# Transfers of a hybrid Mamba, SSD and mixture-of-experts kernel: the experts' reload issued by ScalarE, SSD row loads by quads in one DMA, a pair's decays in one DMA

## The chip, the cores and the metric

The kernel runs on one core of a Trainium2 chip. Its five engines each work through their own list of instructions in order: TensorE (PE in the profile, with its weight loads as PEld), VectorE (DVE), ScalarE (ACT), GpSimd (POOL) and SyncE (SP), which issues most of the DMAs. The metric is the device time of one execution in microseconds; lower is better. Three executions of the kernel before took 849.16, 842.12 and 846.15 us, with a median of 846.15 us.

## The reference

The input x is 4 sequences of 512 tokens with 256 features, all float32. Four blocks follow each other, each with a layer norm in front and its result added to x:

```python
x = x + _L0_attn_a_ref(_layernorm(x, axis=-1), ...)   # selective scan (Mamba), 16 states
x = x + _L0_ffn_ref(_layernorm(x, axis=-1), ...)      # mixture of 8 experts, top 2
x = x + _L0_attn_b_ref(_layernorm(x, axis=-1), ...)   # chunked state-space block (SSD)
x = x + _L0_ffn_ref(_layernorm(x, axis=-1), ...)      # the same mixture, same weights
```

The change lies in the SSD block and in what the last block needs. The SSD block has 64 heads of 8 features and 64 states, and cuts time into chunks of 32:

```python
dA = (dt * A).reshape(b, c, CHUNK, H)
Acs = jnp.cumsum(dA, axis=2)
Lm = jnp.exp(_segsum(jnp.moveaxis(dA, 3, 2)))
Y_diag = jnp.einsum('bclhn,bcshn,bchls,bcshp->bclhp', Ch, Bh, Lm, xd)
decay_states = jnp.exp(Acs[:, :, -1:, :] - Acs)
states = jnp.einsum('bclhn,bclh,bclhp->bchpn', Bh, decay_states, xd)
chunk_decay = jnp.exp(Acs[:, :, -1])
...
_, prev = jax.lax.scan(step, h0, (jnp.moveaxis(chunk_decay, 1, 0), jnp.moveaxis(states, 1, 0)))
Y_off = jnp.einsum('bclhn,bchpn,bclh->bclhp', Ch, prev, jnp.exp(Acs))
```

In the mixture every expert is computed for every token, `h = jnp.einsum('td,edf->etf', xf, expert_w) + expert_b`, then weighted by the router's top two.

## The kernel before, in words

The kernel keeps x in SBUF and runs the four blocks over the four sequences ("batches" b = 0 to 3). In the time of the profile the selective scan fills about the first 320 us, the first mixture (names ending in `_e`) runs beside and after it to about 440 us, the SSD block (names ending in `_s`) from about 440 to 710 us, and the last mixture (`_f`) from there to the end.

**The SSD block.** The heads of a batch are worked in four groups g of 16 heads, and the groups in two pairs p. `front_b` (from L1648) makes for each batch the running sums of the decay exponents (`cs`) and writes the lower rows of both halves to DRAM (`cs_rows`, L1664); it also writes the decays over whole chunks (`dk_rows`, L1680). `weighted` (L1775) then does, for each group: the weighted x is written to DRAM (`x_rows`), and the group's rows of `cs_rows` are read back into a tile `less` in another layout, 16 chunk partitions by 32 steps, two parts of four heads' quads each (L1791 to L1798). `apart` (L1801) reads `x_rows` back, by chunks, in four DMAs into one of two tiles `x_b`. `states` (L1811) does, for each pair: it reads `dk_rows` into two tiles `decays` (one for each half h of a group's heads), each copied to all 64 partitions of a group (L1819 to L1826); TensorE makes the states (`pst`), ScalarE copies them to `starts`, VectorE scans them over the 16 chunks with the decays (`starts<-decays_s_p,starts`), and TensorE multiplies them with C (`po_s_p`). `decayed` makes for each quad q a matmul with `less` (`pe_s`), an exponential and a product (`m_s`); `within` multiplies that with `x_b` (`pz_s<-x_b,m_s`). The tiles `decays` have two buffers in all, so those of a pair are free when the scans of the pair before are done.

**The experts' weights.** The weights of the mixture are split into high and low parts once (`load_moe`), kept in DRAM after the first mixture (`keep_moe`, L849), and read back into the space that the SSD block's front has left, when the front of the last batch is done (`reload_moe`, L858): `expert_h` and `expert_l` of 2 MB each, `expert_b` of 1 MB copied to all partitions, and four small tensors.

**What sets the order.** Every operation is recorded by a planner (class `Plan`, L209 on), which orders all engines' instructions by costs of its own and then issues them; all of them appear as line L612, its last line. It prices a DMA by its bytes alone (`n.cost = max(b / 360e3, 0.112)`, L656), whatever its shape and the number of its pieces. So an edit to a DMA can move instructions all over the program.

**How DMAs are held apart.** The program has eight semaphores for DMAs, given out in turn in the program's order, to SP's and ScalarE's DMAs alike. Before a DMA is issued, its engine waits until the DMA that had the same semaphore before, eight places earlier, has landed. An engine that waits so does nothing else.

Of the kernel before, what the change touches and what calls it, by code (L numbers as in the profile page):

```python
# [22 lines left out]
F32 = mybir.dt.float32  # L23
# [7 lines left out]
P = 128  # L31
# [7 lines left out]
DI, NH, HD, DS = 512, 64, 8, 64  # L39
# [16 lines left out]
BL, NB = 32, P // 32  # L56
# [14 lines left out]
def bc(ap, axis, n):  # L71

    a = ap.unsqueeze(axis)
    shape = list(a.shape)
    shape[axis] = n
    return a.to_broadcast(shape)
# [641 lines left out]
def block(ctx: ExitStack, tc: Plan, a: dict, out: bass.AP):  # L718
    nc = tc.nc
    V, S, G, T = nc.vector, nc.scalar, nc.gpsimd, nc.tensor  # L720
# [22 lines left out]
    def bank(tag, name, shape=(P, L)):  # L743

        if tag == "mm":
            return banks.tile(list(shape), F32, tag=tag, name=name)
        at = turn[tag] = turn.get(tag, -1) + 1
        names = PAIRS.get(tag, tag.split())
        return banks.tile(list(shape), F32, tag=names[at % len(names)], name=name, bufs=1)
# [6 lines left out]
    def load(b):  # L756
# [8 lines left out]
        out=ident, in_=ident, compare_op=ALU.is_equal, fill=0.0, base=0, pattern=[[-1, P]], channel_multiplier=1  # L765
# [49 lines left out]
        S.copy(hi, src)  # L815
        low.tensor_tensor(lo, src, hi.bitcast(F32), ALU.subtract)

    def load_bias(w):
        flat = a["expert_b"].rearrange("e f -> (e f)")
        nc.sync.dma_start(out=w["expert_b"], in_=flat.partition_broadcast(P))  # L820

    def load_moe(w, raw):
        load_bias(w)
# [32 lines left out]
        return kept  # L856

    def reload_moe(w, kept):  # L858
        for key, t in kept.items():
            nc.sync.dma_start(out=w[key].bitcast(F32), in_=t)  # L860
        load_bias(w)

    def row(rows, at, name):
        lo, hi = at[name]
# [253 lines left out]
    for t in range(0, 4, 2):  # L1118
        for k in range(KB):
            nc.scalar.dma_start(  # L1120
                out=conv_w[:, k, t : t + 2], in_=a["conv_w"][t : t + 2, k * P : (k + 1) * P, :].rearrange("t p o -> p t o")
# [8 lines left out]
        out=a_neg.rearrange("p j g -> p (j g)"), in_=a["A_log"].rearrange("(n d) j g -> d n (j g)", d=BL)  # L1130
# [12 lines left out]
    def ltile(shape, name):  # L1143
        return later.tile(shape, F32, tag=name, name=name)
# [26 lines left out]
    for j in range(2):  # L1171
        t = ltile([P, 4, P], f"less_all{j}")
# [3 lines left out]
        flat = t[BL:NH].rearrange("p q c -> p (q c)")  # L1176
# [221 lines left out]
    for b in range(B):  # L1398
# [13 lines left out]
        for k in range(KB):  # L1412
# [3 lines left out]
            for j in range(2):  # L1416
                for r, name in zip(pairs[2 * k + j], "du"):
                    t = m_p.tile([P, 2, L], F32, tag=f"{name}s", name=f"{name}s_{b}_{k}_{j}", bufs=SPREAD)
                    spread.append(t)
                    if b == k == 0:  # L1420

                        for h in range(2):
                            c = slice((2 * j + h) * BL, (2 * j + h + 1) * BL)
# [5 lines left out]
                        out=t.rearrange("p j t -> p (j t)"), in_=bc(r.rearrange("d j t -> d (j t)"), 1, NS)  # L1429
# [61 lines left out]
    at = SSD_AT  # L1491
# [156 lines left out]
    def front_b(b):  # L1648

        nm, small, rot, d_a, zs, xs, wt, ld = made_a.pop(b)  # L1650

        pcs = bank(FRONT_BANKS if b == 0 else "mm", f"pcs_{nm}")
        for i in range(NT):
            T.matmul(
                pcs[:, i * P : (i + 1) * P], d_a[:, i].rearrange("p a c h -> p (a c h)"), upto_b,
                start=True, stop=True,
            )
        cs_rows = dram.tile([2, NH, L], F32, tag="cs_rows", name=f"cs_rows_{nm}")
        cs = c_s[b % 2]
        for a in range(2):  # L1660
            src, lo = pcs[a * NH : (a + 1) * NH], a * NH + NH // 2
            S.copy(cs[a][NH:], src)
            V.tensor_tensor(cs[a][NH + NH // 2 :], pcs[lo : lo + NH // 2], cs[a][NH + NH // 2 :].bitcast(F32), ALU.subtract)
            nc.sync.dma_start(out=cs_rows[a], in_=cs[a][NH:].bitcast(F32))  # L1664
            V.tensor_copy(
                tot[b % 2][a * NH // 2 : (a + 1) * NH // 2, 1:],
                src[: NH // 2].rearrange("p (k l) -> p k l", l=BL)[:, :-1, BL - 1],
            )

        pc = bank(FRONT_BANKS if b == 0 else "mm", f"pc_{nm}")  # L1670
        T.matmul(pc[:, : L // 2], upto_b, d_a[:, :, :, 0, :], start=True, stop=True)
        T.matmul(pc[:, L // 2 :], after_b, d_a[:, :, :, 0, :], start=True, stop=True)
        ends = s_o.tile([P, 2, NT, NH], F32, tag="ends", name=f"ends_{nm}")
        S.activation(ends.rearrange("p c i h -> p (c i h)"), pc, AF.Exp)

        nk = NT * NB
        over_blocks = small("over_blocks", (NH, HD, nk))
        S.activation(over_blocks, bc(tot[b % 2], 1, HD), AF.Exp)
        dk_rows = dram.tile([NH, HD * nk], F32, tag="dk_rows", name=f"dk_rows_{nm}")
        nc.sync.dma_start(out=dk_rows, in_=over_blocks.rearrange("p d k -> p (d k)"))  # L1680
        yield


        nh = NT * NB // 2
        bt = small("rest", (P, L))
        cm = c_m[b % 2]
        for g in range(2):
            pt = bank(FRONT_BANKS if b == 0 else "mm", f"pbc_{nm}_{g}")
            for i in range(NT):
                T.transpose(pt[:, i * P : (i + 1) * P], rot[:, i, g].rearrange("p c n -> p (c n)"), ident)  # L1690
            S.copy(bt if g == 0 else cm, pt)
        bm = b_m[b % 2]
        S.copy(bm, rot[:, :, 0, 0, :])
        gm = s_o.tile([P, nh, 2, BL], F32, tag="gm", name=f"gm_{nm}")
        pg = bank(FRONT_BANKS if b == 0 else "mm", f"pg_{nm}")
        for k in range(nk):
            ks = slice(k * BL, (k + 1) * BL)
            for h in range(4):
                T.matmul(pg[h * BL : (h + 1) * BL, ks], bt[:, ks], cm[:, ks], start=True, stop=True)
        S.activation(gm.rearrange("p j c l -> p (j c l)"), pg, AF.Copy, scale=0.5)  # L1700
        dg = small("tsin", (P, NT, DS))
        V.tensor_tensor(dg, rot[:, :, 0, 0, :], rot[:, :, 1, 0, :], ALU.mult)
        dd = small("dd", (P, NT))
        V.tensor_reduce(dd, dg, AX.X, ALU.add)
        V.tensor_tensor(ld, ld, bc(dd, 2, NH), ALU.mult)
        ready[b] = dict(
            nm=nm, zs=zs, y=xs, wt=wt, ld=ld, ends=ends, dk_rows=dk_rows, gm=gm, cm=cm, bm=bm, cs=cs, cs_rows=cs_rows
        )
# [61 lines left out]
    def per_head(t):  # L1770
        return t.rearrange("p i (h d) -> p i h d", d=HD)
# [3 lines left out]
    def weighted(b, g):  # L1775

        c = ready[b]
        nm = f"{c['nm']}_{g}"
        ch, hs = slice(g * P, (g + 1) * P), slice(g * 16, (g + 1) * 16)
        xs = c["y"][:, :, ch]  # L1780
        xw = pool2.tile([P, NT, P], F32, tag="xw", name=f"xw_{nm}", bufs=1)
        G.tensor_tensor(per_head(xw), per_head(xs), bc(c["wt"][:, :, hs], 3, HD), ALU.mult)
        x_rows = dram.tile([L, P], F32, tag="x_rows", name=f"x_rows_{nm}", bufs=4)
        nc.sync.dma_start(out=x_rows.rearrange("(i p) f -> p i f", p=P), in_=xw)
        xe = pool2.tile([P, NT, P], F32, tag="xe", name=f"xe_{nm}", bufs=XE_BUFS)
        G.tensor_tensor(per_head(xe), per_head(xw), bc(c["ends"][:, 1, :, hs], 3, HD), ALU.mult)

        G.tensor_tensor(per_head(xs), per_head(xs), bc(c["ld"][:, :, hs], 3, HD), ALU.mult)
        nk = NT * NB
        ls = less[g]  # L1790
        for part in range(2):  # L1791
            for q in range(4):
                lo = part * NH // 2 + g % 2 * 16
                src = c["cs_rows"][g // 2, lo + q : lo + 16 : 4, :]
                nc.sync.dma_start(
                    out=ls[part * nk : (part + 1) * nk, q, :].bitcast(F32).rearrange("k (h s) -> k h s", h=4),
                    in_=src.rearrange("h (k s) -> k h s", s=BL),
                )  # L1798
        units[b, g] = dict(xe=xe, x_rows=x_rows, less=ls)

    def apart(b, g):  # L1801
# [9 lines left out]
    def states(b, p):  # L1811

        c = ready[b]
        nm = f"{c['nm']}_p{p}"
        nk = NT * NB
        pair = (2 * p, 2 * p + 1)
        half = [slice(h * DS, (h + 1) * DS) for h in range(2)]
        G.memset(starts[:, :, 0], 0.0)
        decays = []  # L1819
        for h in range(2):  # L1820
            t = pool2.tile([P, P // 2 * nk], F32, tag="decays", name=f"decays_{nm}_{h}")
            for j, g in enumerate(pair):
                at = 16 * g + 8 * h
                src = c["dk_rows"][at : at + 8, :].rearrange("h d -> (h d)")
                nc.sync.dma_start(out=t[half[j]], in_=src.partition_broadcast(DS))
            decays.append(t)  # L1826


        for r0 in range(0, NB, 2):
# [13 lines left out]
            for r in range(r0, r0 + 2):  # L1843
                n = NT if r + 1 < NB else NT - 1
                at = starts[:, :, r + 1 : r + 2 + NB * (n - 1) : NB]
                S.copy(at.rearrange("p c i -> p i c"), pts[r - r0][:, :n, :])
            yield
        for h in range(2):
            at = starts[:, h * P // 2 : (h + 1) * P // 2, :].rearrange("p c k -> p (c k)")
# [83 lines left out]
    order = [(b, g) for b in range(B) for g in range(4)]  # L1933
    coming, going, moe_f, before = [], [], [], None
    weighted(0, 0)
    weighted(0, 1)
    for n, (b, g) in enumerate(order):
# [28 lines left out]
        if g % 2 == 0:  # L1966
            mine = states(b, g // 2)
# [77 lines left out]
```

## Time and profile before

| what | value |
|---|---|
| three executions, median | 846.15 us (842.12 to 849.16) |
| the profiled execution: its time, its span | 836.37 us, 834.7 us |
| PE busy | 709.5 us, 85% of the span |
| DVE busy | 683.8 us, 82% |
| ACT busy | 523.4 us, 63% |
| POOL busy | 527.2 us, 63% |
| granted TensorE clock, mean | 0.894 |
| HBM read and written | 49.67 MB and 16.80 MB |
| less<-cs_rows_s | 128 DMAs of 8 KB, 2.8 us from issue to landing |
| decays_s_p<-dk_rows_s | 32 DMAs of 256 KB, 4.3 us |
| x_b<-x_rows_s | 64 DMAs of 64 KB, 2.4 us |

The profiled execution took 836.37 us; its span, from the first to the last instruction, is 834.7 us. All stretches below are counted from the span's start. In the lists, "SPq" is SP as the issuer of DMAs. A row of a timeline has start, duration, engine, line, operation and tiles, the number of merged instructions, and in brackets the idle time before it and what ended it. A row of the list of waits has who waited, for whom, the total, the number of waits and the longest one, in us. In the list of DMA issues the last number is the median time from issue to landing.

### The profile page before, as it was taken

What the parts mean: (1) busy time and instruction counts of PE and PEld (TensorE: products, weight loads), DVE (VectorE), ACT (ScalarE), POOL (GpSimd) and SP (SyncE); (2) the same over time, 40 slices, a digit from 0 to 9 for tenths busy, and PEclk for the clock granted to TensorE, in tenths of its full rate; (3) what the DMA queues carried; (4) which work ended last, traced back from release to release, by engine and by line L of the source; (5) the groups of instructions that cost most, each with busy time, mean ns of one, the idle gap of its engine ahead of it and who ended that gap; (6) DMA issues with size and microseconds to landing.
All of it is one profiled execution on the core that took longest, in us unless ns stands there. A gap on an engine that the chain in (4) does not pass through costs nothing.

```text
span 834.7 us, 16400 instructions
## 1 busy us (share of the span) xinstructions
PE 709.5 (85%) x6194; PEld 457.5 (55%) x6194; DVE 683.8 (82%) x1278; ACT 523.4 (63%) x965; POOL 527.2 (63%) x410
## 2 busy tenths in 40 slices
PE   8889879966676789799997697789789886999996
PEld 5333324221022247587886475676567664888784
DVE  7488999999999984898996678697677546799987
ACT  2898976865345486566687455645636544686764
POOL 5735857767767574655555886863862873558555
PEclk9989999976577699999999599899789778999999
DMA  8321252241341002600004522521531584000001
GB/s 273 117 76 64 71 184 64 92 162 64 101 176 51 1 7 57 273 1 0 2 5 112 116 64 60 112 65 38 117 80 32 131 264 101 1 1 26 25 2 51
DMA packets 79247, 67.55 MB, mean 81 GB/s; under 512 B 48696, under 2 KB 66040, under 8 KB 78400
## 3 DMA queue, kind: packets, MB, share of 16 engines
q1 hardware_dynamic: 77664, 65.35, 27.2%
q10 hardware_dynamic: 1504, 1.15, 0.5%
q8 instruction: 49, 0.80, 0.4%
q14 instruction: 30, 0.25, 0.1%
HBM read 49.67 MB, written 16.80 MB: 80 GB/s over the span
## 4 chain that ended last, share of the span: by engine, by line
PE 35%; DVE 15%; ACT 8%; SPq 5%; issue 5%; POOL 3%; DMA 1%; POOLq 0%; ACTq 0%; DVEq 0%
PE ph_e L612 8%; PE ph_f L612 6%; SPq L612 5%; PE pz_s L612 4%; DVE hs L612 3%; PE px_s L612 3%; PE po_s L612 2%; DVE starts L612 2%; PE pst_s_p L612 2%; DVE bx L612 1%; PE po_s_p L612 1%; ACT L610 1%; ACT ph_e L612 1%; PE pe_s L612 1%; DVE ph_f L612 1%
## 5 line engine op out<-in xcount | busy, mean ns | idle before, releaser
L612 POOL TENSOR_TENSOR hs<-hs,cb 128x1024 f32<-128x1024 f32 x64 | 151.8, 2380 | 73.8 <-DVE hs L612 61.1
L612 DVE TENSOR_TENSOR_SCAN hs<-da,bx 128x512 f32<-128x512 f32 x128 | 150.5, 1213 | 8.3 <-ACT da L612 5.8
L612 ACT ACTIVATE da<-ds,a_neg 128x512 f32<-128x512 f32 x128 | 87.5, 689 | 76.8 <-DVE hs L612 76.6
L612 PE MATMUL ys<-hs,over 128*32 128x512 f32 x256 | 73.7, 755 | 27.9 <-POOL hs L612 27.9
L612 DVE TENSOR_TENSOR bx<-us,pb 128x1024 f32<-128x1024 f32 x64 | 76.3, 1211 | 0.2
L612 POOL TENSOR_TENSOR m_s<-m_s,gm_s 128x512 f32<-128x512 f32 x32 | 45.3, 1421 | 32.8 <-ACT m_s L612 32.7
L610 ACT ACT_TABLE_LOAD x51 | 65.4, 1283 | 0.9
L612 PE MATMUL pconv<-hh,conv 128*128 128x512 f32 x128 | 60.8, 622 | 1.1 <-ACT hh L612 1.1
L612 ACT ACTIVATE ph_f<-ph_f 128x512 f32<-128x512 f32 x64 | 37.5, 588 | 26.9 <-DVE ph_f L612 26.6
L612 DVE TENSOR_TENSOR ph_f<-ph_f,expert_b 128x512 f32<-128x512 f32 x64 | 43.9, 694 | 11.7 <-DMA expert_b<-in_expert_b_dram 5.7
L612 ACT ACTIVATE ph_e<-ph_e 128x512 f32<-128x512 f32 x64 | 36.8, 586 | 23.7 <-DVE ph_e L612 15.9
L612 PE MATMUL ph_e<-expert_h,xs_of_xh_e 128*128 128x512 f32 x128 | 44.9, 413 | 4.2 <-ACT c_e L612 4.2
L612 PE MATMUL pe_s<-c_s,less 128*128 128x512 f32 x64 | 32.9, 544 | 16.2 <-DMA less<-cs_rows_s 7.4
L612 PEld LDWEIGHTS ys<-hs,over 128*32 128x32 f32 x256 | 8.8, 118 | 66.9 <-POOL hs L612 51.9
L612 POOL TENSOR_TENSOR c_e<-c_e,hb_e 128x512 f32<-128x512 f32 x16 | 20.6, 1290 | 36.1 <-ACT hb_e L612 36.1
L612 PEld LDWEIGHTS pconv<-hh,conv 128*128 128x128 f32 x128 | 24.1, 196 | 34.4 <-issue 28.1
L612 ACT COPY starts<-pst_s_p 128x512 f32<-128x512 f32 (+1 forms) x32 | 29.6, 1010 | 18.3 <-PE pst_s_p L612 18.3
L612 PE MATMUL pz_s<-x_b,m_s 128*32 128x32 f32 x2048 | 31.9, 216 | 10.0 <-DMA x_b<-x_rows_s 5.7
L612 DVE TENSOR_TENSOR_SCAN starts<-decays_s_p,starts 128x1024 f32<-128x1024 f32 x16 | 38.9, 2439 | 1.5 <-issue 1.3
L612 PEld LDWEIGHTS pz_s<-x_b,m_s 128*32 128x32 f32 x2048 | 26.3, 127 | 23.4 <-issue 15.3
L612 PE MATMUL ph_f<-expert_h,xh_f 128*128 128x512 f32 x96 | 38.4, 400 | 0.7 <-ACT c_f L612 0.7
L612 PE MATMUL ph_f<-expert_l,xh_f 128*128 128x512 f32 x96 | 38.4, 400 | 0.0
(399 smaller groups left out, 2163.2 us busy)
## 6 DMA issues: line engine op xcount, KB each, us to landing
decays_s_p<-dk_rows_s SPq DMA_DIRECT2D x32, 256.0 KB, 4.3
ds<-d_rows SPq DMA_DIRECT2D x14, 512.0 KB, 3.8
us<-u_rows SPq DMA_DIRECT2D x14, 512.0 KB, 3.9
cb<-c_rows SPq DMA_DIRECT2D x16, 256.0 KB, 3.3
x_rows_s<-xw_s SPq DMA_DIRECT2D x16, 256.0 KB, 3.0
x_b<-x_rows_s SPq DMA_DIRECT2D x64, 64.0 KB, 2.4
x<-in_x_dram SPq DMA_DIRECT2D x4, 512.0 KB, 4.7
raw_expert<-in_expert_w_dram SPq DMA_DIRECT2D x4, 512.0 KB, 7.1
```

Of the source, the lines that this page charges most:

```text
L610: self.real.scalar.preload_act_table_set(n.table)
L612: n.inst = f(*[self.swap(v) for v in n.args], **{k: self.swap(v) for k, v in n.kw.items()})
```

## The change

There are three edits. The reload of `expert_h`, `expert_l` and `expert_b` goes from SP to ScalarE, in ScalarE's own DMA queue; the four other tensors of the reload stay on SP. The rows of `cs_rows` are written in another order, by four DMAs of 16 rows where there was one of 64, so that the read into `less` takes one DMA for a part where it took four. A pair's decays for one half are read by one DMA into all 128 partitions, where there were two of 64 partitions.

```diff
-    def load_bias(w):
+    def load_bias(w, queue=nc.sync):
         flat = a["expert_b"].rearrange("e f -> (e f)")
-        nc.sync.dma_start(out=w["expert_b"], in_=flat.partition_broadcast(P))
+        queue.dma_start(out=w["expert_b"], in_=flat.partition_broadcast(P))
...
     def reload_moe(w, kept):
+
         for key, t in kept.items():
-            nc.sync.dma_start(out=w[key].bitcast(F32), in_=t)
-        load_bias(w)
+            (S if "expert" in key else nc.sync).dma_start(out=w[key].bitcast(F32), in_=t)
+        load_bias(w, S)
...
-            nc.sync.dma_start(out=cs_rows[a], in_=cs[a][NH:].bitcast(F32))
+
+            for at in range(0, NH, 16):
+                nc.sync.dma_start(
+                    out=cs_rows[a, at : at + 16].rearrange("(q h) l -> h q l", h=4),
+                    in_=cs[a][NH + at : NH + at + 16].bitcast(F32),
+                )
...
         for part in range(2):
-            for q in range(4):
-                lo = part * NH // 2 + g % 2 * 16
-                src = c["cs_rows"][g // 2, lo + q : lo + 16 : 4, :]
-                nc.sync.dma_start(
-                    out=ls[part * nk : (part + 1) * nk, q, :].bitcast(F32).rearrange("k (h s) -> k h s", h=4),
-                    in_=src.rearrange("h (k s) -> k h s", s=BL),
-                )
+            lo = part * NH // 2 + g % 2 * 16
+            nc.sync.dma_start(
+                out=ls[part * nk : (part + 1) * nk].bitcast(F32).rearrange("k q (h s) -> k (q h) s", s=BL),
+                in_=c["cs_rows"][g // 2, lo : lo + 16, :].rearrange("h (k s) -> k h s", s=BL),
+            )
...
             t = pool2.tile([P, P // 2 * nk], F32, tag="decays", name=f"decays_{nm}_{h}")
-            for j, g in enumerate(pair):
-                at = 16 * g + 8 * h
-                src = c["dk_rows"][at : at + 8, :].rearrange("h d -> (h d)")
-                nc.sync.dma_start(out=t[half[j]], in_=src.partition_broadcast(DS))
+            src = c["dk_rows"].rearrange("(g c h) d -> g c (h d)", c=2, h=8)[2 * p : 2 * p + 2, h]
+            nc.sync.dma_start(out=t, in_=bc(src, 1, DS))
             decays.append(t)
```

The new decays DMA has as its source 2 rows, each repeated 64 times, of 1,024 elements; its destination has 128 partitions of 1,024. In the built program the planner puts nearly every engine's instructions in another order than before, from the second sequence of the first block on.

## The prediction

> **What bounds the kernel now.** I read first the page's chain of work that ended last, then the time by stretch, one for each batch of the SSD block, then who waited for which DMA, then the DMA issues, and at last single stretches of the timelines. The chain is mostly TensorE (35%) and VectorE (15%), with SP as issuer at 5%, some 45 us. Work per batch of the SSD block:
>
> ```profile
> 440.00:505.00 65.00, 50.87 (x856) 38.86 (x856) 43.10 (x86) 38.64 (x73) 46.59 (x38) 0.84 0.42 95
> 505.00:573.00 68.00, 56.07 (x1141) 44.71 (x1140) 57.91 (x88) 37.60 (x73) 45.30 (x37) 0.92 0.31 69
> 573.00:640.00 67.00, 56.78 (x1016) 43.11 (x1016) 48.27 (x77) 36.70 (x69) 39.22 (x33) 0.87 0.33 73
> 640.00:710.00 70.00, 56.63 (x1232) 42.70 (x1231) 37.85 (x74) 35.95 (x61) 45.24 (x37) 0.80 0.59 157
> ```
>
> After the length, these columns begin with PE's busy time. PE is busy 51 to 57 of 65 to 70 us in each batch: it is the stage's bound, with 10 to 14 us idle per batch. Only that idle time can be won by faster transfers, and it has several owners. The list of waits gives what the edited DMAs and `x_b` behind them cost PE, and what SP's own big loads cost SP:
>
> ```profile
> PE pe_s L612 <- DMA less<-cs_rows_s: 7.4, 4, 5.8
> PE pz_s L612 <- DMA x_b<-x_rows_s: 5.7, 3, 2.9
> ...
> SPq L612 <- DMA expert_l<-kept_expert_l: 5.4, 1, 5.4
> SPq L612 <- DMA expert_h<-kept_expert_h: 4.9, 1, 4.9
> ```
>
> So 13.1 us of PE's idle time ends on a DMA of SP's queue; 45 us of the chain is SP only because the chain goes back through a queue in which PE's work hides most.
>
> **Row loads by quads.** They take 128 issues of 427 ns (median of the tile's view); 32 remain, so 96 x 0.47 us (with the gap between two) = 45 us of SP time go. The writes of `cs_rows` rise from 8 to 32, 24 x 0.5 = 12 us. The 16 decays issues that go had a median of 574 ns: 9 us. SP wins 42 us, 10 per batch, in the bursts ahead of `x_b`. On the path that is at most the 13.1 us above, of which 5.8 (the longest) belongs to the last batch and the experts' loads; I count a gain of 6 us in batches 0 to 2 and put the rest into the last batch. The new read has 256 runs of 128 bytes, half of an `x_b` read's 512, which takes 487 ns to issue and lands in 2.4 us: no loss there.
>
> **The decays in one DMA.** This is where I expect the loss.
>
> ```profile
> q1 hardware_dynamic: 77664, 65.35, 27.2%
> ...
> decays_s_p<-dk_rows_s SPq DMA_DIRECT2D x32, 256.0 KB, 4.3
> ...
> us<-u_rows SPq DMA_DIRECT2D x14, 512.0 KB, 3.9
> ```
>
> (The q1 row is SP's queue: packets, MB, share of 16 engines.) What no row shows is a DMA of this form: outermost count 2 in the source, 128 in the destination. Lower bound: it is spread like `us`, also 512 KB, 3.9 us. Upper bound: few DMA engines carry it. The trace records each DMA engine's update of a DMA's semaphore. DMAs whose outermost counts are 16 or more (`cb`: 32 in the source, 128 in the destination) leave 16 updates. The two DMAs of four rows, at 23.7 and 33.5 us, leave five: one right at the issue and four at the landing. So the number of engines follows the outermost count, and I take 2. A DMA engine's price for 4 KB: q1 used 0.272 x 16 x 834.7 = 3,633 engine us for 65.35 MB, 55.6 us per MB, so 0.262 MB (half of 512 KB) takes 14.6 us; the faster half of the packets of 4,096 bytes took 159 ns, and 64 of them 10.2 us. With 2 us from issue to landing as for a small DMA: 12 to 17 us instead of 4.3. I take 12, since the rest of the queue is light.
>
> The Trainium skill speaks on both sides here. "DMA: Bandwidth & Descriptors", in the section "Why a DMA increments its semaphore by 16 and not by 1", says that the largest number up to 16 that divides the outermost counts of both sides is the number of engines, which makes the decays use 2 and leaves the sum as it is here. The same page, in "Rules for kernel authors", says of two transfers to disjoint halves of the partitions "Use one 128-partition transfer", by which the edit could only win and the sum would be that of the first rival below.
>
> The scans themselves have room. In batch 1 the decays were issued from 526.26 to 530.29 and the first scan began at 542.86:
>
> ```profile
> 542.86 2.82 DVE L612 TENSOR_TENSOR_SCAN starts<-decays_s_p,starts 128x1024 f32<-128x1024 f32 x1
> ```
>
> The two DMAs of a pair share the two engines, so the second lands 2 + 2 x 10.2 = 22.4 us after the first's issue. That the scans bear within 0 to 3 us. What they do not bear is everything behind the decays in SP's queue: a sixteenth of each `x_rows`, `x_b` and `less` DMA goes over the same two engines and stands in line. PE takes `x_b` as it lands:
>
> ```profile
> 537.79 0.45 PE L612 MATMUL pz_s<-x_b,m_s 128*32 128x32 f32 x16 [2.11 <-DMA x_b<-x_rows_s]
> ```
>
> By batch, with the new order of SP's queue and the old times:
>
> - Batch 0: decays now stand after the second `x_rows` (issued at 466.18) and before the second `x_b`. They are issued at 466.7 and end at 489; PE used that `x_b` from about 475. Loss 13 us.
> - Batch 1: a decays DMA stands on each side of `x_rows` of group 2, which POOL has ready at 527.6. The second ends at about 541, `x_b` lands at 543; it was used at 537.8. Loss 5 us.
> - Batch 2: both stand before that `x_rows`. With the shorter queue they are issued at about 587 and end at 609.4; `x_b` lands 2.4 us later at 611.8, and was used at 605.14. Loss 7 us.
>
> **The experts' reload on ScalarE.** The three issues cost ACT 3 x 0.43 us. The wait costs more. By the eight semaphores in turn, `expert_b` has that of `expert_l`, so ACT stands until `expert_l` has landed. The trace shows that time on SP:
>
> ```profile
> 665.55 0.43 SPq L612 DMA_DIRECT2D expert_h<-kept_expert_h  x1
> ...
> 666.59 0.42 SPq L612 DMA_DIRECT2D expert_l<-kept_expert_l  x1
> 667.05 2.61 SPq L612 DMA_DIRECT2D less<-cs_rows_s  x5
> 674.65 1.09 SPq L612 DMA_DIRECT2D decays_s_p<-dk_rows_s  x2
> 681.17 1.71 SPq L612 DMA_DIRECT2D less<-cs_rows_s  x4
> ```
>
> SP stood at 669.7 for `expert_h` and at 675.7 for `expert_l`, 15.6 us from the first issue to 681.17. ACT will stand for those 15 us with this queued behind: a copy `yh_s`, an exponential of `pe_s`, one of `m_s` and the first copies of `starts`. PE can go on with some 4 us (the output product of a tile of batch 2 and one or two `pe_s`), then it stands too: 10 to 12 us. SP is not freed either: a `cs_rows` write now has the semaphore of `expert_h`. Behind it in SP's queue stand the other decays of the pair, issued some 20 us after the first, so they land 12 us later still. The pair's first scan, at 662.97 before, ends up at about 686. For the second pair `x_b` of group 3 stands between the two decays: PE is through `po_s_p` and `pz_s` of the last pair at about 725 where it was at 706.8, with some 3 us more of `ph_f` done by then. I take 15 us for the last batch, everything counted, the 5.8 us that go included. The last mixture keeps PE busy 56 of the last 65 us, so nothing is made up there.
>
> **The sum.** 13 + 5 + 7 + 15 = 40 us, less 6 for the shorter queue, less 6 because after each stall some of PE's other idle time is gone (VectorE and POOL have run ahead): +28 us. The moved order of the first 440 us I count at nothing; it could be some 6 us either way, a tenth of PE's 66 idle us there. The profiled execution of 836.37 us would become 864; the median of 846.15, 10 us above it, becomes 874.
>
> **Rivals.** (1) Faster: the decays DMA is spread over all 16 engines. Then it lands in about 5 us, all 13 us of PE's waits go, and the stand of ACT is covered by PE's queue: 846 - 13 = 833 us. It decides if a decays DMA lands within some 6 us. For it speaks the `us` row; against it the four-row DMAs. (2) No change: the decays are slow, but the two engines take turns between DMAs, so `x_b` lands in 4 or 5 us, and the scans' room covers the decays. Then the loss is ACT's stand, 10 us, against 10 won: 846 us, 840 to 853. For it speaks the room of 8 us and more ahead of most scans; against it, that `x_b` waits on the decays only if each engine works in order of issue, which no row shows. (3) Worse: at 14.6 us for each half of a decays DMA, a pair takes 31 us where a pair's time is 33. Then scans and `x_b` are both late by 9 us more in each batch: 874 + 31 = 905 us.
>
> **Chances.** Forecast 0.68, rival 1 0.07, rival 2 0.13, rival 3 0.12. A measurement of this kernel can't tell less than about 1% from no change, so faster means under 838 and slower over 854.5 us: 0.07, 0.13 and 0.80. The forecast's own range, with the bounds of the batches' losses, is 856 to 895. To leave out no more than 2 in 10 the range goes from 848, the middle of rival 2, to 903, the near end of rival 3.
>
> **What will show it.** In the profile after, a decays DMA's time to landing should be 12 us or more, and `x_b`'s longest well over the 8.9 us of before. PE's waits for `x_b` or for what stands before it should grow to 20 us or more. ACT should have one gap of about 15 us just after the issue of `expert_l`. SP should have 32 `less` issues and more time in waits than in issues. I would be wrong if decays land in 4 to 6 us, or if ACT's gap falls where PE has work, or if the new order by itself moves the first 440 us by more than 6 us.

## The result, and the profile after

The changed kernel takes 906.81 us (median of 6 runs, 903.57 to 911.64), the kernel before 844.31 us beside it (median of 6). The ratio is 1.0748, with a 95% interval of 1.0695 to 1.0801: 62.5 us slower. The forecast was 874 us, with a range of 848 to 903. The direction was right, the size was not, and the time lies above the range.

The page of the changed kernel: its first line, the busy times, and the shares of the chain that ended last, by engine and by line:

```profile
span 906.5 us, 16309 instructions
...
PE 725.8 (80%) x6194; PEld 466.8 (51%) x6194; DVE 690.1 (76%) x1278; ACT 529.1 (58%) x967; POOL 531.7 (59%) x410
...
PE 35%; DMA 17%; DVE 9%; ACT 5%; issue 3%; POOL 3%; SPq 2%; POOLq 0%; DVEq 0%; ACTq 0%
PE ph_f L612 9%; PE ph_e L612 9%; DMA x_rows_s<-xw_s 8%; DMA decays_s_p<-dk_rows_s 4%; PE pz_s L612 3%; DVE hs L612 3%; DMA raw_W_out<-in_W_out_dram 3%; PE px_s L612 2%; SPq L612 2%; DMA x_b<-x_rows_s 2%; PE po_s L612 2%; DVE starts L612 1%; ACT L610 1%; DVE bx L612 1%; PE pj_f L612 1%
```

The chain has changed its owner. SP as issuer has gone from 5% to 2%, and DMAs in flight, 1% before, hold 17%, some 154 us. The largest share among them is not `x_b`'s (2%) but that of the writes of `x_rows` (8%). TensorE's busy time has grown by only 16 us (709.5 before): what has grown is the waiting.

The time by stretch, cut at the end of each batch's last `pz_s<-x_b`, first of the kernel before, then of the changed one. After the length come the busy times of PE, PEld, DVE, ACT and POOL, then the granted TensorE clock, the DMA share and GB/s:

```profile
440.00:513.90 73.90, 57.35 (x1125) 44.29 (x1125) 51.90 (x95) 44.80 (x85) 53.61 (x43) 0.84 0.41 92
513.90:584.20 70.30, 59.03 (x1155) 45.65 (x1156) 55.49 (x89) 38.60 (x72) 44.26 (x39) 0.95 0.30 69
584.20:646.70 62.50, 53.69 (x942) 41.61 (x942) 45.63 (x74) 34.32 (x66) 36.53 (x30) 0.86 0.34 76
646.70:706.80 60.10, 48.01 (x1015) 36.17 (x1011) 32.11 (x61) 29.34 (x49) 40.99 (x33) 0.77 0.64 172
```

```profile
440.00:522.70 82.70, 55.09 (x968) 40.68 (x966) 47.03 (x86) 38.71 (x72) 46.19 (x38) 0.79 0.29 74
522.70:611.80 89.10, 61.83 (x1088) 48.21 (x1088) 52.87 (x91) 41.89 (x78) 47.05 (x36) 0.77 0.24 62
611.80:692.00 80.20, 60.34 (x1171) 47.43 (x1170) 54.71 (x81) 39.14 (x71) 43.31 (x35) 0.82 0.22 59
692.00:779.50 87.50, 52.27 (x1023) 39.05 (x1023) 38.88 (x66) 34.83 (x56) 37.61 (x32) 0.70 0.40 120
```

The four batches are longer by 8.8, 18.8, 17.7 and 27.4 us, 72.7 us together; the last mixture behind them takes 127.0 us where it took 127.9. (The profiled execution of before was 8 us faster than its median, so the traces differ by 71.8 us and the medians by 62.5.) The DMA share falls in every batch and the rate with it: no more is moved (67.55 MB in both), it takes longer.

The list of waits of the changed kernel (who waited, for whom, total, number, longest):

```profile
POOL xw_s L612 <- DMA x_rows_s<-xw_s: 46.3, 6, 23.5
...
PE pz_s L612 <- DMA x_b<-x_rows_s: 42.2, 5, 17.2
...
ACT yh_s L612 <- DMA expert_l<-kept_expert_l: 15.7, 1, 15.7
...
PE po_s L612 <- ACT yh_s L612: 13.4, 2, 12.9
...
DVE starts L612 <- DMA decays_s_p<-dk_rows_s: 12.3, 2, 10.5
```

TensorE waits 42.2 us for `x_b`, 5.7 before. The first line was not in the forecast: POOL waits 46.3 us for writes of `x_rows` (4.7 before), because the tile `xw` that they read has one buffer, so the next group's `xw_s` can't begin until the write has landed.

The list of DMA issues gives no time to landing for this kernel. It can be had from the trace, where each DMA engine's update of a semaphore is recorded: the landing is the last update of a DMA's semaphore before the next DMA with that semaphore is issued. In this way (times from the start of the issue):

```
                     before                        changed kernel
decays    32 DMAs, median  4.2, longest  7.7   16 DMAs, median 15.6, longest 27.3
x_rows    16 DMAs, median  2.6, longest  4.3   16 DMAs, median  3.9, longest 27.4
x_b       64 DMAs, median  2.4, longest  8.9   64 DMAs, median  2.8, longest 20.0
updates left by a decays DMA:   16             3, the first some 0.9 us after the issue, two at the landing
```

A decays DMA that has its engines to itself lands 12.2 us after its issue, and of a pair issued at 582.87 and 586.92 the second lands 22.4 us after the first's issue. The forecast had 12 and 22.4. SP's queue in batch 2 shows what that does to its neighbours (start, duration, merged instructions), and TensorE's row the price:

```profile
623.97 3.74 SPq L612 DMA_DIRECT2D decays_s_p<-dk_rows_s  x2
628.07 5.01 SPq L612 DMA_DIRECT2D x_rows_s<-xw_s  x1
647.32 1.90 SPq L612 DMA_DIRECT2D x_b<-x_rows_s  x4
```

```profile
651.18 0.33 PE L612 MATMUL pz_s<-x_b,m_s 128*32 128x32 f32 x8 [12.96 <-DMA x_b<-x_rows_s]
```

The two decays land at 636.4 and 646.6, and `x_rows`, 256 KB issued behind them, at 647.3. Only then can the `x_b` reads be issued; they land within 2 to 3 us, at 651.05, and TensorE has waited 13 us for them. It is the write that was late, not the read. The write's updates show which engines held it: of its 16, 14 came 6.7 to 7.2 us after the issue and the last two after 19.2, when the decays had landed. In batch 1 both were late: `x_rows`, issued at 543.70, lands at 556.2 behind the first decays, and the reads issued from 556.25 on stand behind the second, which land at 567.7; the reads land at 567.9 to 568.8. There, too, 14 of the write's updates came within 4.6 us and two after 12.5.

Other DMAs behind the decays pay as well. In batch 0 a load of output weights, `raw_W_out`, issued at 465.38, lands 23.1 us later and holds ScalarE for 17.2 us. And SP itself is held: from 440 us on, 19 of its issues take over 2 us, 91 us together (one before, 3.5 us), as the 5.01 us of the `x_rows` row above and 8.65 us at 465.38. No run separates what SP's long issues cost from what the late landings cost.

The late write has a second way to TensorE. The rows of POOL, DVE and PEld from 556 us on:

```profile
556.34 1.07 POOL L612 TENSOR_TENSOR xw_s<-xs_s,wt_s 128x512 f32<-128x512 f32 x1 [9.48 <-DMA x_rows_s<-xw_s]
557.37 1.26 POOL L612 TENSOR_TENSOR xs_s<-xs_s,off_s_p 128x512 f32<-128x512 f32 x1
...
558.66 0.69 DVE L612 TENSOR_TENSOR xs_s<-pz_s,xs_s 128x512 f32<-128x512 f32 x1 [10.11 <-POOL xs_s L612]
...
559.40 0.75 PEld L612 LDWEIGHTS pz_s<-x_b,m_s 128*32 128x32 f32 x35 [9.11 <-DVE xs_s L612]
```

POOL stood 9.5 us until the write had landed, with an addition to `xs_s` queued behind `xw_s`; DVE stood for that addition, with the sum that empties `pz_s` behind it; and TensorE stood for `pz_s`. The list of waits puts TensorE's 8.9 us here down to `x_b`, but those reads had landed at 543.8, 15 us earlier: of its 42.2 us, 8.9 belong to the write of `x_rows` by way of POOL.

### The profile page after: what moved, and what is told of

Its sections match the earlier page's. It is cut to its first block, busy times and chain, and to the rows that moved or that the text cites. A ratio compares the mean times of both kernels' runs of the same rounds, so it can differ in the third digit from the quotient of the medians.

```text
span 906.5 us, 16309 instructions
## 1 busy us (share of the span) xinstructions
PE 725.8 (80%) x6194; PEld 466.8 (51%) x6194; DVE 690.1 (76%) x1278; ACT 529.1 (58%) x967; POOL 531.7 (59%) x410
## 2 busy tenths in 40 slices
DMA packets 77231, 67.55 MB, mean 75 GB/s; under 512 B 46680, under 2 KB 64024, under 8 KB 76384
## 4 chain that ended last, share of the span: by engine, by line
PE 35%; DMA 17%; DVE 9%; ACT 5%; issue 3%; POOL 3%; SPq 2%; POOLq 0%; DVEq 0%; ACTq 0%
PE ph_f L612 9%; PE ph_e L612 9%; DMA x_rows_s<-xw_s 8%; DMA decays_s_p<-dk_rows_s 4%; PE pz_s L612 3%; DVE hs L612 3%; DMA raw_W_out<-in_W_out_dram 3%; PE px_s L612 2%; SPq L612 2%; DMA x_b<-x_rows_s 2%; PE po_s L612 2%; DVE starts L612 1%; ACT L610 1%; DVE bx L612 1%; PE pj_f L612 1%
## 5 line engine op out<-in xcount | busy, mean ns | idle before, releaser
L612 PE MATMUL pz_s<-x_b,m_s 128*32 128x32 f32 x2048 | 31.6, 218 | 43.6 <-DMA x_b<-x_rows_s 42.2
L612 PE MATMUL pconv<-hh,conv 128*128 128x512 f32 x128 | 62.8, 640 | 0.5 <-ACT hh L612 0.5
L612 POOL TENSOR_TENSOR xw_s<-xs_s,wt_s 128x512 f32<-128x512 f32 x16 | 21.5, 1342 | 62.7 <-DMA x_rows_s<-xw_s 46.3
L612 DVE TENSOR_TENSOR m_s<-pe_s,gm_s 128x512 f32<-128x512 f32 x32 | 21.8, 680 | 34.7 <-ACT pe_s L612 25.2
L612 ACT ACTIVATE pe_s<-pe_s 128x512 f32<-128x512 f32 x32 | 19.3, 604 | 46.2 <-PE pe_s L612 46.0
```

The lines of the kernel that those rows point to most:

```text
L612: n.inst = f(*[self.swap(v) for v in n.args], **{k: self.swap(v) for k, v in n.kw.items()})
```

## The experiments

In all of them "A" is the theory of the forecast: the decays DMA is carried by two DMA engines and holds up what is behind it in SP's queue. Each time stands beside the kernel before on the same chip: 841.08 us for the first four, 838.33 for the next four, 840.46 for the last four.

### Each part by itself

**The changed kernel with two decays DMAs.**

```diff
-            src = c["dk_rows"].rearrange("(g c h) d -> g c (h d)", c=2, h=8)[2 * p : 2 * p + 2, h]
-            nc.sync.dma_start(out=t, in_=bc(src, 1, DS))
+            for j, g in enumerate(pair):
+                at = 16 * g + 8 * h
+                src = c["dk_rows"][at : at + 8, :].rearrange("h d -> (h d)")
+                nc.sync.dma_start(out=t[half[j]], in_=src.partition_broadcast(DS))
```

> The changed kernel with the decays again in two DMAs of 64 partitions; quads and the reload on ScalarE stay. Theory A (the decays in one DMA are carried by two DMA engines and hold up every transfer behind them in SP's queue): a decays DMA lands in 3.5 to 6 us again, and the time is 835 to 858 us, so at least 50 of the 62 us that the change cost are gone. Theory B (the reload on ScalarE and its wait in the last batch are the main loss): the time stays above 870 us. Theory C (the planner's new order of all engines is the loss): above 870 us too, with decays that land quickly.

Measured: 834.04 us, ratio 0.9924 (0.9886 to 0.9963), 1 us under A's range. The whole loss is gone and 7 us more. Decays land in 4.4 us (median), and the waits for `x_b` and `x_rows` are back at 1.2 and 2.8 us. Theories B and C fall as explanations of the main loss.

**The decays in one DMA alone**, on the kernel before (the same lines, the other way).

> The kernel before with only the decays in one DMA for two. Theory A: 885 to 910 us, with 12 us from issue to landing for a decays DMA that is alone and about 22 us for the second of a pair. Batches 1 and 3 should lose most again, as an x_rows write and the x_b read that needs it each stand behind a decays DMA. Theory B: 840 to 855 us. Theory C: anything; it would show as a loss in batches where no transfer waits behind decays.

Measured: 923.76 us, ratio 1.0966 (1.0902 to 1.1029), above A's 885 to 910. By itself the edit costs 82.7 us, more than all three together: with 128 reads of `less` instead of 32 in the same queue, more of them stand behind the decays. From the list of waits of this kernel:

```profile
PE pz_s L612 <- DMA x_b<-x_rows_s: 40.4, 4, 16.2
PE pe_s L612 <- DMA less<-cs_rows_s: 35.6, 11, 10.0
```

In the changed kernel the second line was 6.6 us. The batches lose 18.4, 19.7, 4.2 and 46.8 us.

**The rows by quads alone**, on the kernel before (the `cs_rows` and `less` parts of the change's diff).

> The kernel before with only the rows by quads (32 reads of less, 32 writes of cs_rows). Theory A: a gain of 0 to 13 us, so 831 to 844 us, since less and x_b were awaited by TensorE for 13 us in all. Rival: SP's issues were never what TensorE waited for, and the time is that of before within 4 us; or the writes of 16 rows in four DMAs delay the less reads, and it is 850 us or more.

Measured: 832.87 us, ratio 0.9882 (0.9823 to 0.9941), a gain of 8.2 us. PE's wait for `x_b` falls from 5.7 to 2.8 us and for `less` from 7.4 to 2.1 us. It is the part of the change that keeps its promise, as far as this goes: the planner's order changed with it, and the order alone moved the time as far the other way (8.1 us, below). The edit has a side that the forecast did not see: the four writes of `cs_rows` leave 5 updates each where the one write left 16, so they, too, run on four engines. At 16 rows each that costs nothing by itself: they land in 2.0 us (median in the changed kernel), the one write in 2.3.

**The experts' reload on ScalarE alone**, on the kernel before.

```diff
-            nc.sync.dma_start(out=w[key].bitcast(F32), in_=t)
-        load_bias(w)
+            (S if "expert" in key else nc.sync).dma_start(out=w[key].bitcast(F32), in_=t)
+        load_bias(w, S)
```

> The kernel before with only the reload of the experts' weights issued by ScalarE. Theory A: ScalarE has one wait of 10 to 16 us for expert_l or expert_h, of which TensorE pays at most 10: 844 to 856 us. Theory B: above 870 us. Rival to both: ScalarE's wait falls where TensorE has other work, and SP is freed of its 10 us of waits for expert_h and expert_l: 832 to 842 us.

Measured: 866.99 us, ratio 1.0292 (1.0229 to 1.0355), 25.9 us slower: between A's 856 and B's 870. ScalarE's timeline in the last batch shows the stand that the forecast described:

```profile
671.06 0.35 ACTq L612 DMA_DIRECT2D expert_h<-kept_expert_h  x1
...
680.76 0.35 ACTq L612 DMA_DIRECT2D expert_l<-kept_expert_l  x1
689.51 0.34 ACTq L612 DMA_DIRECT2D expert_b<-in_expert_b_dram  x1
689.95 0.59 ACT L612 CAST yh_s<-pyt_s 128x512 fp32r<-128x512 f32 x1 [17.31 <-DMA expert_l<-kept_expert_l]
```

The 17.3 us are two waits: until 680.7 for `moe_rows`, a load of SP's that had the semaphore of `expert_l` before it, and until 689.5 for `expert_l`, whose semaphore `expert_b` has. TensorE waits for the copies behind it: its waits of `po_s` for `yh_s` sum to 15.8 us, the longest 13.5. The last batch loses 19.5 us of this kernel's 31.4 (by the traces). The rest arose in batches 0 to 2, where only the planner's order differs; see the last two experiments. (The traced execution of before was some 5 us faster than the median beside this kernel, and that is in the rest too.) With two decays DMAs and quads (the first experiment) the same reload cost nothing: 834.04 against 832.87 us without it. There the three were issued as `expert_l`, `expert_b`, `expert_h`, `expert_b` had another semaphore and was issued 0.4 us after `expert_l`, and ScalarE's longest wait for a semaphore in that place was 3.9 us. So by these two kernels, whether this edit costs TensorE 13 us hangs on which semaphores fall to its DMAs; the order differs between them as well.

### How many engines

**One decays DMA from 16 rows.** Each of the two rows is first copied eight times in DRAM, and the decays' source is 16 rows, each repeated 8 times.

```diff
+        dk_rep = dram.tile([2, 32, HD * nk * 8], F32, tag="dk_rep", name=f"dk_rep_{nm}")
+        for e in range(2):
+            nc.sync.dma_start(
+                out=dk_rep[e].rearrange("(g r) x -> g r x", r=8),
+                in_=bc(dk_rows.rearrange("(g c h) d -> g c (h d)", c=2, h=8)[:, e], 1, 8),
+            )
...
-            src = c["dk_rows"].rearrange("(g c h) d -> g c (h d)", c=2, h=8)[2 * p : 2 * p + 2, h]
-            nc.sync.dma_start(out=t, in_=bc(src, 1, DS))
+            step = 1
+            src = c["dk_rep"][h, 16 * p : 16 * p + 16 : step]
+            nc.sync.dma_start(out=t, in_=bc(src, 1, 8 * step))
```

> The changed kernel, still with one decays DMA of 512 KB for both groups, but its source is now 16 rows of 4 KB in DRAM (each of the two rows in eight copies, written by two more DMAs of 128 KB per batch), each repeated 8 times, where it was 2 rows repeated 64 times. Same bytes, same destination. Theory A (the outermost count of the source sets the number of DMA engines): 16 semaphore updates in place of 3, landing in 4 to 6 us, and a time of 830 to 848 us, near that of the kernel with two decays DMAs (834 us). Rival (a DMA of 128 partitions from so few rows is slow by itself, or one of 512 KB is): landing stays above 10 us and the time above 885 us.

Measured: 850.3 us, ratio 1.0133 (1.0075 to 1.0191), 2 us above A's 848. A decays DMA leaves 16 updates and lands in 4.2 to 6.9 us, but for one that ran beside the experts' weights (11.0).

**2, 4, 8 and 16 rows**, by batch: `step = 8 >> b` in the same kernel, so that batch b takes every eighth, fourth, second or each row.

> The same as the kernel with copies, but the decays' source has 2 rows in batch 0, 4 in batch 1, 8 in batch 2 and 16 in batch 3, repeated 64, 32, 16 and 8 times; the writes are the same in all batches. Theory A: 3, 5, 9 and 16 semaphore updates, and for a decays DMA with nothing beside it 2 + (128 rows / engines) x 0.159 us to land: 12.2, 7.1, 4.5 and 3.3 us, the last two perhaps 4 us as for the other DMAs of 512 KB. Rival: about 12 us in all four batches, or one step between 2 and the rest.

Measured: 875.66 us in its one execution. The shortest landing of a decays DMA in each batch, the updates that it left, and the batch's loss against the kernel with 16 rows, which has the same order of instructions on every engine:

```
rows = engines        2        4        8        16
landing, us        12.4      8.7      6.3       4.5
formula, us        12.2      7.1      4.5       3.3
updates               3        5        9        16
batch's loss, us   15.2     11.6      1.5       1.5
```

The number of engines is the outermost count of the source, as A says, and the loss falls with it. It is not a matter of which batch: with 2 rows in all of them (the next experiment) the same batches lose 18.5, 20.0, 10.4 and 15.1 us. The Trainium skill's "DMA: Bandwidth & Descriptors", section "Why a DMA increments its semaphore by 16 and not by 1", says that k engines post one update each and the issuer adds the rest at once. With one record for the rest, and none where k is 16, that makes 3, 5, 9 and 16, the counts of this table. The formula's price for a row of 4 KB, 159 ns, holds for two engines only: the landing less 2 us, divided by each engine's rows, is 163, 209, 269 and 312 ns.

**2 rows in all batches**: `step = 8`.

> The kernel with copies and one decays DMA, but the decays' source takes 2 of the 16 rows, each repeated 64 times, in all four batches. Against the kernel that takes 16 rows (850 us) nothing differs but the source's pattern: the order of all engines' instructions, the queues and the bytes are the same. Theory A (two engines for the decays are the whole of the loss by that edit): a decays DMA lands in 12.4 us or more, each batch loses 12 to 17 us as batch 0 did in the kernel with 2, 4, 8 and 16 rows, and the time is 900 to 918 us. Rival 1 (batch 3 loses more, 25 us or more, as the experts' weights run beside its decays): 915 to 930 us. Rival 2 (much of the loss in the changed kernel is its order, not the engines): under 885 us.

Measured: 909.62 us, ratio 1.0837 (1.0788 to 1.0886), inside A's range and 59.3 us more than with 16 rows and the same order. This is the cleanest price of the two engines: nothing differs but the source's pattern. The lists of waits of the kernel with 16 rows and of the one with 2:

```profile
POOL xw_s L612 <- DMA x_rows_s<-xw_s: 19.2, 3, 17.2
...
PE pz_s L612 <- DMA x_b<-x_rows_s: 3.5, 2, 2.1
```

```profile
PE pz_s L612 <- DMA x_b<-x_rows_s: 46.3, 6, 13.0
...
POOL xw_s L612 <- DMA x_rows_s<-xw_s: 33.1, 4, 24.1
```

In the traces the batches lose 18.5, 20.0, 10.4 and 15.1 us, 64.0 together, or pair by pair 11.3, 7.2, 8.7, 11.3, 1.8, 8.6, 8.2 and 6.9 us: 8 us per pair on average, and each pair pays. (A had 12 to 17 for each batch; the sum holds, the shares spread wider.) SP's issues over 2 us, from 440 us on, are none with 16 rows and 17 with 2, 69.5 us together. Rival 1 of this run, a last batch that pays 25 us or more for its decays, falls.

**Quads, one decays DMA from 16 rows, the reload on SP**: the kernel with 16 rows, with `reload_moe` and `load_bias` as before.

> Quads, the reload on SP, and one decays DMA for both groups from 16 rows of copies, so that it uses 16 engines. If one decays DMA in place of two is worth its 9 us of SP's issues: 822 to 831 us, faster than quads alone (833 us). If SP's issues are no longer awaited, or the two more writes per batch cost as much: 831 to 845 us.

Measured: 848.89 us, ratio 1.0109 (1.0051 to 1.0168), above both forecasts. Even with all 16 engines one DMA for two is no gain here: with two DMAs of 64 partitions this kernel is the one with quads alone, 832.87 us. The copies' writes and another order are in the difference and were not told apart.

### Another queue

**The changed kernel with the reload on SP** (`reload_moe` and `load_bias` as before).

> The changed kernel with the reload of the experts' weights issued by SP as before; quads and the decays in one DMA stay. In the changed kernel the first decays DMA of the last batch took 27.3 us, beside 4 MB of experts' weights in ScalarE's queue, and the batch lost 41 us. Theory D (weights in a queue of their own share the decays' two engines and hold them up): the last batch loses 12 to 20 us less, and the time is 885 to 895 us. Rival (in SP's queue the weights are in front of the decays or behind them, with the same loss): 900 to 915 us, about 8 us under the kernel with only the decays in one DMA (924 us).

Measured: 912.62 us, ratio 1.0874 (1.0819 to 1.093). The rival holds. (The 41 us named above for the last batch, and the 32 in the next forecast for batches 0 to 2, were read with other cuts between the batches; by the ends of `pz_s<-x_b` they are 27.4 and 45.3.) On SP the weights stand in the same queue as the last pair's decays, which land 22.4 and 29.9 us after their issue, and the `x_b` behind them after 29.1 us. This kernel loses 74.3 us, the changed one 62.5, so beside slow decays the reload on ScalarE looks the better place; of these 12 us the order may hold a part.

**The decays issued by ScalarE.**

```diff
-            nc.sync.dma_start(out=t, in_=bc(src, 1, DS))
+            S.dma_start(out=t, in_=bc(src, 1, DS))
```

> The changed kernel with the one decays DMA issued by ScalarE, so it is in another queue than x_rows, x_b and less; it still uses two DMA engines. Theory E (an engine takes turns between queues, and works within one queue in order): x_rows and x_b issued while decays are in flight land in 2 to 6 us, batches 0 to 2 lose at most 10 us together in place of 32, and the time is 850 to 885 us, with what ScalarE's own waits cost. Rival (an engine works in order of issue whatever the queue, or ScalarE's waits for semaphores cost as much): x_rows and x_b still land 10 us late or more, and the time is 890 us or more.

Measured: 903.19 us, ratio 1.0748 (1.0694 to 1.0802). Theory E falls: the queue of its own changes little. (ScalarE's waits are in this time too: one of 19.0 us for a `less` read whose semaphore `expert_b` had, with 14.7 us of TensorE behind it.) SP's and ScalarE's timelines in batch 1 (start, duration):

```profile
533.74 8.29 SPq L612 DMA_DIRECT2D x_b<-x_rows_s  x4
```

```profile
532.75 1.21 ACTq L612 DMA_DIRECT2D decays_s_p<-dk_rows_s  x2
```

The decays land at 546.4 and 557.0, and the four `x_b` at 545.7, 551.1, 556.5 and 557.2. Of each `x_b`'s 16 updates two come late, the others within 8.1 us: these are the two engines that the decays use. The queues do take turns there, but a turn is long: one 64 KB read of SP's gets through per 5.3 to 5.4 us. At the 163 ns per row of the table above that is about 33 of the 64 rows that each of the two engines carries for a decays DMA (an estimate from these two numbers).

### The order by itself

**The kernel before with the planner's price of a DMA at 330 and at 390 kB per us.**

```diff
-        n.cost = max(b / 360e3, 0.112)
+        n.cost = max(b / 330e3, 0.112)
```

> The kernel before, with only the planner's price of a DMA changed (330 kB per us in place of 360), so that it puts the same instructions in another order. If the order by itself moves the time by less than 6 us, as was forecast: 832 to 846 us beside 838 to 841 us of the kernel before. Rival (the order by itself explains most of the 26 us that the reload on ScalarE alone cost): 850 us or more in one of this and the next kernel, or a spread of 15 us between the two.

> The same with a price of 390 kB per us. As for the kernel before it in this list: 832 to 846 us if the order by itself is worth less than 6 us, 850 us or more if it explains the reload's 26 us.

Measured: 848.6 us, ratio 1.0105 (1.0074 to 1.0136), and 842.83 us, ratio 1.0022 (0.999 to 1.0054). An order that the planner finds without any change of work cost 8.1 and 2.4 us. The first lies between the two ranges of the forecast, the second in the lower one. So an order can cost as much as part of what the reload alone lost in batches 0 to 2, though not all of its 25.9 us; how much of that was order remains open. It also means that differences of 8 us between kernels of unlike order, above, are not shown to be the edit's own.

## Why the prediction was wrong

**The mechanism was right as far as it went.** Two engines, 12 us for a decays DMA, 22 us for a pair, `x_b` late behind them in SP's queue, one stand of ScalarE of 15 us (15.7 measured): the steps that were to show it right are all in the profile after. Rival 1 (spread over 16 engines) and rival 2 (turns between DMAs that let `x_b` through in 4 or 5 us) fall by the 3 updates and the 12 us landings. Rival 3 named 905 us, next to the result, for a reason that did not occur: half a decays DMA took the 10.2 us of the forecast, not 14.6. (Its sum is also off: 9 us more in each of four batches is 36, where it added 31.)

**The term that was mis-sized is the batches' loss by the decays: "13 + 5 + 7".** It followed one late `x_b` per batch. There are two pairs in each batch, and each pays: 18.5, 20.0 and 10.4 us for batches 0 to 2 with the order held, 48.9 us where the forecast had 25. What it missed was in its own list of transfers that stand in line: it named `x_rows` there, and then followed `x_b` alone. The write behind the first decays, the reads that need it behind the second, and POOL's next `xw_s`, which waits for the write because `xw` has one buffer, each take their own time; in the chain that ended last `x_rows` has 8% and `x_b` 2%. In the changed kernel batches 0 to 2 lost 8.8, 18.8 and 17.7 us.

**"15 us for the last batch, everything counted"** was 27.4 us. The stand of ScalarE was forecast well: TensorE was to stand 10 to 12 us and stood 12.9, as this row of the changed kernel shows.

```profile
715.67 0.58 PE L612 MATMUL po_s<-W_out_h,yh_s 128*128 128x256 f32 x1 [12.93 <-ACT yh_s L612]
```

But that stand is not on the chain that ended last. In the list of that chain in order of time (start, length) the stretch belongs to a write of `x_rows`:

```profile
698.49 27.35 DMA x_rows_s<-xw_s
```

It was issued right behind the decays (697.85) and the experts' weights in ScalarE's queue (698.03 and 698.42). Of its 16 updates 14 come 12.6 to 13.4 us after the issue, where 2.2 is usual, and the last two after 27.0 and 27.4: so all engines were some 10 us late beside the weights, and the two of the decays 14 us later still. After ScalarE's stand TensorE worked for 8.1 us and then stood again, 4.6 us, for POOL, which had waited for this write:

```profile
725.98 1.07 POOL L612 TENSOR_TENSOR xw_s<-xs_s,wt_s 128x512 f32<-128x512 f32 x1 [23.54 <-DMA x_rows_s<-xw_s]
```

So most of the 12.9 us looks hidden behind the late write, and no run shows what the batch would take without them. In the kernel with 2 rows from copies ScalarE has no such stand (SP stands there for the weights, 12.4 us, ahead of this write), and its last batch loses 26.7 us against the kernel before all the same: 11.6 with 16 engines and 15.1 by the two.

**"Less 6 because after each stall some of PE's other idle time is gone" is not borne out.** With the order held TensorE's busy time grew by 10.3 us behind the stalls (see the clock below), a term of the other sign that the forecast did not have; whether its other idle time shrank was not measured by itself. "Less 6 for the shorter queue" came out near: quads alone gave 8.2 us, and 8.4 us beside the slow decays (82.7 - 74.3), each with another order, which alone can move as much.

**"The moved order I count at nothing"** was about right for the time ahead of the SSD block (the first block's last `hs`, at 310.8 us before, moves by -1 to +5 us between the traces), but not for the SSD block: one of two trials cost 8.1 us, and in its trace the first batch of that block ends 1.6 us late and the last 11.8.

**The sum again.** The two engines cost 59.3 us with the order held, and 69.5 us as the step from two decays DMAs to one with the other two edits in both (from -7.0 to +62.5, the order included); the forecast had 25 in batches 0 to 2, and what it gave the decays in the last batch was part of the 15. So the decays in one DMA are the loss, and the rest (quads, reload, order) comes to between +3 and -7 us, depending on which of the two prices is taken. The three parts tried alone (+82.7, +25.9, -8.2) sum to 100 us: they don't add up, since the slow decays cost more where more reads stand behind them, and the reload's price hangs on semaphores and on what else is late.

Of the chances, 0.80 for slower by over 1% was right. The best version found is the kernel with the quads alone, 832.87 us, 1.2% under the kernel before; the one with the reload on ScalarE besides, 834.04 us, is not told apart from it.

## What to carry to other kernels

Before two DMAs are merged into one, look at the outermost counts of both sides: here a merge took a transfer from 16 engines to 2, and its own delay was the smaller part of the price. Price a slow DMA by every transfer that comes behind it on those engines, once for each repetition, and follow each to the producer that waits for its buffer; a write and the read that needs it pay one after the other. Where a list of waits names a DMA, compare its landing: if it had landed long before, another engine was waited for. When a compute engine issues DMAs, look which semaphore each gets: a DMA that waits for the one eight places before it stops all that engine's work.

## What the runs showed of the hardware

**TensorE ran slower behind a stall.** Matmuls of one shape before and after the 12.9 us stand in the changed kernel:

```profile
700.78 0.28 PE L612 MATMUL po_s<-W_out_h,yl_s 128*128 128x256 f32 x1
...
716.94 0.41 PE L612 MATMUL po_s<-W_out_h,yh_s 128*128 128x256 f32 x1
...
734.14 0.41 PE L612 MATMUL po_s<-W_out_l,yh_s 128*128 128x256 f32 x1
```

The time by stretch of the changed kernel has the granted clock in the third column from the end:

```profile
690.00:702.00 12.00, 10.51 (x240) 8.07 (x244) 7.32 (x17) 6.67 (x16) 11.10 (x10) 0.72 0.51 127
...
715.00:735.00 20.00, 13.87 (x148) 12.12 (x149) 5.48 (x9) 7.27 (x12) 7.61 (x7) 0.50 0.34 104
```

The clock was 0.50 for 20 us after the stand, in which TensorE was busy 69% of the time and the same matmul took 0.41 us where it had taken 0.28. Over the kernels with 16 and with 2 rows, whose instructions are the same in the same order, TensorE's busy time goes from 716.4 to 726.7 us: 10.3 of the 64.0 us between their traces are longer busy time, not waits. The Trainium skill's "TensorE: Matmul & The Clock Gate", "Part 1: The HAM clock gate", says that an idle window of some 3.4 us throttles the clock to half, and that about 3.4 us of sustained work releases it. The half clock behind the stand agrees; the release does not at first: the rows show TensorE at work without a gap from 715.67 to 723.76, 8.1 us (the ends of matmuls are modelled), and the clock stayed at 0.50. It was full again from 735.0 on, 4.5 us after work began anew at 730.53.

**A queue of its own is no way past a slow transfer.** In the kernel with the decays in ScalarE's queue, two queues on the same two DMA engines took turns of about 5.3 us, so three reads of 64 KB in a row landed 12, 17 and 22 us after their issue.
